# v with pixels on partitions, pixel blocks turned on VectorE, and another pacing of the taps in an attention and involution kernel

## The chip, the cores and the metric

One NeuronCore of a Trainium2 chip runs the kernel; the other cores are idle. The metric is the device time of one execution in microseconds. The engines are TensorE (PE), VectorE (DVE), ScalarE (ACT), GpSimd (POOL) and SyncE (SP), which here only issues DMAs. They run in parallel, each through its own list of instructions in order.

## What is computed

Two layers on an image batch of 4 x 512 channels x 64 x 64 pixels in fp32. The first is self-attention over the 4096 pixels of an image with 128 channels for q, k and v. The second is an involution, a 7x7 convolution whose weights are made per pixel and are shared by groups of 16 channels.

```python
# layer 0
q = einsum('oc,bcn->bon', wq, x) + bq        # 128 x 4096 per image, k and v alike
attn = softmax(einsum('bci,bcj->bij', q, k), axis=-1)
x = einsum('oc,bcn->bon', wo, einsum('bcj,bij->bci', v, attn)) + bo + x
# layer 1
o1 = relu(conv1x1(x, W1) * s1 + b1)          # 512 -> 128 channels
w  = conv1x1(relu(conv1x1(o1, Wr) * sr + br), Ws) + bs    # 49 taps x 8 groups per pixel
o2[c] = sum over 49 taps of w[tap, group of c] * (o1 shifted by the tap)[c]
x = conv1x1(o2, W3) * s3 + b3 + x
```

## The kernel before

**Layout.** Channels stand on partitions. An image is worked in eight chunks of 512 pixels (8 rows of 64). `fast_path` does all the work. `general_path`, which is built into the program too, runs only if the softmax sums leave a safe range, and isn't touched.

**Keys and values** (`keys_values`, L420). Once for each image, chunks 2 to 7, then 1 and 0. PE makes `pk` with four 512-column matmuls of the k weights on x, and ScalarE writes it to `kt` with the bias. PE makes `pv` in the same way, with channels on partitions; ScalarE copies it to `vs`; one chunk later `turn` lets PE transpose it in four pieces (`pvt`), and ScalarE copies that to `vT`, which has pixels on partitions as the second attention matmul needs it. The bias of v is added to the output bias (`bo`) instead.

**Attention** (`attention`, L576). For each block of 512 queries, 32 steps: a score matmul of 512 columns (`pss`), exp on ScalarE into one of five `pt` buffers, a value matmul into `po`, and DVE's sum of the `pt` into `pacc` in PSUM. The score runs two steps ahead. The last chunk of the last image is worked in two halves.

**After a block** (`finish_block`, L473). DVE makes the row sums, PE spreads them (`pl`), DVE scales; four matmuls `pwo` (L511) with the residual addition on DVE (L513); then `p1` from the sum, `o1` on ScalarE. `o1` is transposed on PE in four pieces (`pp`, L541), copied to `o1t`, and written to a DRAM scratch `pix` with two DMAs (L548), pixels by channels with zero margins. `pr` and `red` are the input of the involution's weights. The block adds two units of four image rows to `units`.

**The involution** (`involution`, L280). The `ring` in SBUF holds twelve image rows, loaded from `pix` by `pump` (L219) with two DMAs for each group of rows, seven shifted copies of a row side by side. For a unit, PE makes the weights (`pw`), DVE multiplies ring rows by weights (`prod`, L330, four buffers), and GpSimd adds into `acc` (L354). An operation takes n = 1 to 4 of the seven tap rows at once. `turn_unit` transposes the sum (`pa`), and `close_chunk` makes `py` and adds it to x on DVE (L408), after which x goes out. In the tail, after the last attention step, PE takes every second addition (`accp`), since it has nothing else to do.

**What sets the order.** A planner written out in the kernel. It counts PE's time in `pe` (`PE_COLUMN` for each column) and estimates when the others are free in `free`. `finish_block`, `turn_unit`, `close_chunk` and `involution` are generators. `chores` (L248) runs after every two matmuls of k or v and after every attention step, which is about 1.7 us of PE. It moves one step in `finishing`, one in `closing`, and then calls `pace` (L212), which places tap operations as long as PE's time has earned them (1.56 tap rows per us, not more than two operations a call). A tap operation is put off while the planned times of DVE or GpSimd lie too far ahead of PE's (3.5 and 7.5 us, L310) or while the ring rows it needs are not planned to have landed. A wait in a generator is a `yield`. All DMAs but one are issued by SP, and a scheduler places them between each other.

**The lead-in.** SP loads the k weights, then the first chunk of x in four parts, then the v weights; ScalarE loads the small vectors (L171). GpSimd sets `ones` (L180).

Of the kernel before, what the change touches and what calls it, by code (L numbers as in the profile page):

```python
# [8 lines left out]
F32 = mybir.dt.float32  # L9
# [4 lines left out]
B, C, H, W = 4, 512, 64, 64  # L14
N = H * W
P = 128
# [52 lines left out]
DVE_TAPS, POOL_TAPS = (0.16, 0.27), (0.19, 0.55)  # L69
ROW_US, X_US, PIX_US, LAND_US = 2.2, 3.8, 1.5, 3.0  # L70
HOP_US = 0.8
TB = 32

SAFE = (1e-30, 1e20)

# [2 lines left out]
def fast_path(  # L78
# [69 lines left out]
    reds, sums_c = {}, {}  # L148
    written = {}
    landing = {}  # L150
    low, load = 0, 0

    def until(us):
# [3 lines left out]
    def pe_us(us):  # L157
        nonlocal pe
        pe += us
# [8 lines left out]
        nc.sync.dma_start(xs[b, c], x_r[b, :, :, c * CH : (c + 1) * CH])  # L168


    nc.scalar.dma_start(vec, vecs)  # L171
    nc.sync.dma_start(wt[:, :O_WV], wts[:, :O_WV])
    c0, c1 = KEYS[:2]
    xs = {(0, c0): xpool.tile([P, CT, CH], F32, tag="x", name=f"x_0_{c0}")}
    for t in range(CT):
# [1 line left out]
    nc.sync.dma_start(wt[:, O_WV:O_WQ], wts[:, O_WV:O_WQ])  # L177
    load_x(0, c1)
    nc.sync.dma_start(wt[:, O_WQ:], wts[:, O_WQ:O_WR])
    nc.gpsimd.memset(ones, 1.0)  # L180
    make_identity(nc, ident)
    nc.gpsimd.memset(zero, 0.0)
    for i in range(P // TB):
# [8 lines left out]
    def w_slice(off, t):  # L192
        return wt[:, off + t * P : off + (t + 1) * P]
# [17 lines left out]

    def pace():  # L212
        nonlocal due, seen
        due, seen = min(due + TAPS_A_US * (pe - seen), 20), pe
        for _ in range(2):
            if due < 2 or not step(taps, 1):
                break

    def pump():  # L219

        nonlocal load
        while load // STEP in written:
            b, row = divmod(load, STEP)
            rows, us = written[b]

            end = H + SR - UR if rows == H else rows + PAD - 1
            n = min(b * STEP + end, low + RING) - load
            n = min(n, RING - load % RING)
            if n <= 0:
                break  # L230
            for h in range(2):
                src = pix[b % 2][row + h : row + h + n, :W, :]
                windows = bass.AP(
                    tensor=src.tensor, offset=src.offset, ap=[[P, W], [WP * P, n], [1, K * P]]
                )
                nc.sync.dma_start(
                    ring[h * W : (h + 1) * W, load % RING : load % RING + n]
                    .rearrange("p r x c -> p r (x c)"),
                    windows,
                )  # L240
            free["dma"] = max(free["dma"], us)
            us = takes("dma", ROW_US * n) + LAND_US
            landing.update((load + i, us) for i in range(n))
            load += n
            if row + n == H + SR - UR:
                load = (b + 1) * STEP
# [33 lines left out]
    def involution():  # L280
        nonlocal low, due
        while True:
# [15 lines left out]
            for o, (x, dy, n) in enumerate(ops):  # L298
                if o and dy >= DYS[1][0] > ops[o - 1][1]:
                    low = base + UR  # L300
                    pump()
                    if tail and units:
                        early[units[0]] = weights(*units[0])
                rows = [(base + dy + t * 2) % RING for t in range(NT)]
                while base + dy + n + NT > load:
                    yield "wait"
                landed = max(landing[base + dy + i] for i in range(n + NT))
                while not tail and (
                    pe < max(begin, landed)
                    or free["dve"] > pe + 3.5  # L310
                    or free["pool"] > pe + 7.5
                ):
                    yield "wait"
                free["pool"] = max(free["pool"], takes("dve", DVE_TAPS[0] + DVE_TAPS[1] * n))
                takes("pool", POOL_TAPS[0] + POOL_TAPS[1] * n)
                due -= n
                d0 = dy - DYS[dy >= DYS[1][0]][0]
                first = x == 0 and dy < DYS[1][0]
                prod, p0 = acc, d0
                if not first:  # L320
                    prod, p0 = prods.tile(
                        [P, NT, 4, P], F32, tag="prod", name=f"prod_{b}_{u}_{o}"
                    ), 0
                col = (x * K + dy) * G
                lines = ring[:, rows[0] : rows[0] + n, x, :]
                image = bass.AP(
                    tensor=lines.tensor, offset=lines.offset,
                    ap=[lines.ap[0], [(rows[1] - rows[0]) * K * P, NT], [K * P, n], [1, P]],
                )
                nc.vector.tensor_tensor(  # L330
                    prod[:, :, p0 : p0 + n, :].rearrange("p t d (g c) -> p t d g c", g=G),
                    image.rearrange("p t d (g c) -> p t d g c", g=G),
                    pw[:, :, col : col + n * G].unsqueeze(3)
                    .broadcast_to([P, NT, n * G, GC])
                    .rearrange("p t (d g) c -> p t d g c", d=n),
                    ALU.mult,
                )
                if first:
                    pass
                elif tail and o % 2 and (accp is not None or n > 1):  # L340

                    begin_sum = accp is None
                    if begin_sum:
                        accp = ps1.tile(
                            [P, NT, 2, P], F32, tag=("po", "acc")[u % 2], name=f"accp_{b}_{u}"
                        )
                    for d in range(0, n, 2):
                        k = min(2, n - d)
                        mm(
                            accp[:, :, :k, :], ident, prod[:, :, d : d + k, :],  # L350
                            begin_sum and d == 0, o + 2 >= len(ops) and d + 2 >= n,
                        )
                else:
                    nc.gpsimd.tensor_tensor(  # L354
                        acc[:, :, d0 : d0 + n, :], acc[:, :, d0 : d0 + n, :], prod[:, :, :n, :],
                        ALU.add,
                    )
                yield
# [61 lines left out]
    def keys_values(b):  # L420
        kt = kvpool.tile([P, N], F32, tag="k", name=f"k_{b}")
        vT = kvpool.tile([P, N // P, P], F32, tag="v", name=f"v_{b}")

        def turn(c, vs):
            pvt = ps1.tile([P, 4, P], F32, tag="acc", name=f"pvt_{b}_{c}")
            for j in range(4):
                nc.tensor.transpose(pvt[:, j, :], vs[:, j * P : (j + 1) * P], ident)
            pe_us(0.5)
            nc.scalar.copy(vT[:, 4 * c : 4 * c + 4, :], pvt)

        last = None
        for i, c in enumerate(KEYS):
            for k in KEYS[i + 1 : i + 3]:
                if (b, k) not in xs:
# [12 lines left out]
            nc.scalar.activation(  # L447
                kt[:, c * CH : (c + 1) * CH], pk, AF.Identity, bias=v1(V_BK)
            )
            if last is not None:  # L450
                turn(*last)
            pv = ps1.tile([P, CH], F32, tag="po", name=f"pv_{b}_{c}")
            for t in range(CT):
                mm(pv, w_slice(O_WV, t), xt[:, t, :], t == 0, t == CT - 1)
                if t % 2:
                    chores()
            vs = work2.tile([P, CH], F32, tag="q", name=f"vs_{b}_{c}")
            nc.scalar.copy(vs, pv)
            last = c, vs
        turn(*last)  # L460
        return kt, vT

    def queries(b, c, off, n):
# [9 lines left out]
    def finish_block(b, c, off, n, po, sums):  # L473
# [35 lines left out]
        for t in range(CT):  # L509
            pw = ps.tile([P, CH], F32, tag="mm", name=f"pwo_{name}_{t}")[:, :n]  # L510
            mm(pw, w_slice(O_WO, t), on)  # L511
            takes("dve", DVE_OP * n / CH)
            nc.vector.scalar_tensor_tensor(  # L513
                xt[:, t, :], pw, bo[:, t : t + 1], xt[:, t, :], ALU.add, ALU.add
            )
            for _ in range(t % 2 if late else 1 + (t != 1)):
                yield
        p1 = ps.tile([P, CH], F32, tag="mm", name=f"p1_{name}")[:, :n]
        for t in range(CT):
            mm(p1, w_slice(O_W1, t), xt[:, t, :], t == 0, t == CT - 1)  # L520
# [5 lines left out]
        def last_bias():  # L526

            for t in range(CT):
                nc.scalar.activation(xt[:, t, :], xt[:, t, :], AF.Identity, bias=v1(V_B3 + t))  # L529
                if t % 2:  # L530
                    yield

        if late:
            yield from until(pe + HOP_US)
        else:
            yield from last_bias()

        tiles = n // P
        pp = ps.tile([P, CH // P, P], F32, tag="mm", name=f"pp_{name}")[:, :tiles]
        for t in range(tiles):  # L540
            nc.tensor.transpose(pp[:, t, :], o1[:, t * P : (t + 1) * P], ident)  # L541
        pe_us(0.5)
        o1t = work1.tile([P, CH // P, P], F32, tag="o1t", name=f"o1t_{name}")[:, :tiles]
        nc.scalar.copy(o1t, pp)
        top = c * RW + off // W
        for h in range(2):
            row = PAD + top + h
            nc.sync.dma_start(  # L548
                pix[b % 2][row : row + 2 * tiles - 1 : 2, PAD : PAD + W, :]
                .rearrange("r w c -> w r c"),  # L550
                o1t[h * W : (h + 1) * W],
            )
        us = takes("dma", PIX_US) + LAND_US

        pr = ps.tile([P, CH // NT], F32, tag="mm", name=f"pr_{name}")[:, : n // NT]
# [77 lines left out]

    taps = [involution()]
    for b in range(B):
        kv = keys_values(b)
        if b == 0:

            pb = ps.tile([P, CT], F32, tag="mm", name="pb")
# [412 lines left out]
```

## Time and profile before

| | us |
|---|---|
| median of 14 runs | 2659.97 |
| lowest and highest | 2654.53, 2663.03 |
| the profiled execution | 2660.41 |
| its span, first to last instruction | 2658.6 |
| mean granted TensorE clock | 0.996 |

The stretches of the span, from the trace. The four attention stretches are long and even; between them lie the image changes, in which k and v of the next image are made while the last blocks of the old one are finished.

| stretch, us | what | PE busy | DVE busy | POOL busy |
|---|---|---|---|---|
| 0 to 66 | k and v of image 0 | 60.86 | 0.00 | 2.66 |
| 66 to 625 | attention 0 | 558.60 | 384.91 | 338.08 |
| 625 to 702 | change to image 1 | 74.57 | 40.95 | 64.21 |
| 702 to 1268 | attention 1 | 566.00 | 419.64 | 404.41 |
| 1268 to 1350 | change to image 2 | 78.94 | 42.85 | 67.03 |
| 1350 to 1912 | attention 2 | 562.00 | 416.61 | 400.69 |
| 1912 to 1998 | change to image 3 | 81.51 | 43.78 | 69.23 |
| 1998 to 2555 | attention 3 | 556.60 | 417.91 | 402.24 |
| 2555 to 2658.6 | end | 89.50 | 81.33 | 66.67 |

How to read it: an fp32 matmul shows as two records (x2 in the lists), each with a weight load of its own on the line PEld. Matmuls are pipelined and the length of one record includes its drain, so the time a matmul costs is the distance to the next one's start and not its length. Idle time of an engine stands in brackets, with the instruction whose end released it.

### The profile page before, as it was taken

How to read it: one execution, taken by the hardware profiler on the slowest of the kernel's cores; microseconds unless marked ns; L12 is line 12 of the kernel's file. 1: busy time of each engine (PE TensorE's matmuls, PEld its weight loads, DVE VectorE, ACT ScalarE, POOL GpSimd, SP SyncE). 2: the span in 40 equal slices, each digit the busy share in tenths (PEclk: the TensorE clock that was granted, in tenths of full speed). 3: DMA queues.
4: the chain of work that ended last, by engine and by line, in shares of the span. 5: the costliest groups of instructions: out<-in, count | busy, mean ns of one | idle time of the engine just before them, and what ended most of it. 6: DMA issues, size and time to landing. Idle time of an engine off the chain costs nothing.

```text
span 2658.6 us, 22780 instructions
## 1 busy us (share of the span) xinstructions
PE 2628.6 (99%) x6834; PEld 1200.0 (45%) x6834; DVE 1848.0 (70%) x2601; ACT 886.5 (33%) x1486; POOL 1815.2 (68%) x1195
## 2 busy tenths in 40 slices
PE   9999999999999999999999999999999999999998
PEld 4444444444444444444444444444444444444574
DVE  0347788786665777778565678778747577777877
ACT  2333333332333333333233333333323333333330
POOL 0007788788852878878774487878778277888865
PEclk9999999999999999999999999999999999999999
DMA  6032322235604233333440433333452423322243
GB/s 231 0 73 60 90 69 76 61 71 137 159 32 105 60 91 91 91 91 78 126 127 20 89 72 76 91 91 91 107 153 70 105 60 91 78 57 58 56 99 99
DMA packets 104259, 231.59 MB, mean 87 GB/s; under 512 B 5240, under 2 KB 23872, under 8 KB 104000
## 3 DMA queue, kind: packets, MB, share of 16 engines
q1 hardware_dynamic: 103984, 229.96, 35.1%
q8 instruction: 55, 0.90, 0.1%
q14 instruction: 76, 0.62, 0.1%
q10 hardware_dynamic: 144, 0.10, 0.0%
HBM read 187.28 MB, written 42.77 MB: 87 GB/s over the span
## 4 chain that ended last, share of the span: by engine, by line
PE 91%; POOL 4%; DMA 2%; DVE 2%; issue 1%; SPq 0%; ACT 0%; POOLq 0%; DVEq 0%; ACTq 0%
PE pss L200 33%; PE po L200 33%; PE p L200 4%; PE py L200 4%; PE pwo L200 4%; PE pq L200 4%; POOL acc L354 4%; PE pv L200 2%; PE pk L200 2%; PE pw L200 2%; DMA ring<-pix 1%; DVE prod L330 1%; PE accp L200 1%; PE pr L200 1%; DMA out_dram<-x 1%
## 5 line engine op out<-in xcount | busy, mean ns | idle before, releaser
L354 POOL TENSOR_TENSOR acc<-acc,prod 128x768 f32<-128x768 f32 (+3 forms) x1060 | 1693.3, 1616 | 818.1 <-DVE prod L330 632.9
L200 PE MATMUL pss<-q,k 128*128 128x512 f32 (+1 forms) x2112 | 1059.0, 586 | 0.0
L200 PE MATMUL po<-pt,v 128*128 128x512 f32 (+1 forms) x2112 | 1047.2, 580 | 0.0
L594 ACT ACTIVATE pt<-pss 128x512 f32<-128x512 f32 x1024 | 611.2, 597 | 1226.3 <-PE pss L200 1198.4
L625 DVE TENSOR_TENSOR pacc<-pacc,pt 128x512 f32<-128x512 f32 x958 | 666.2, 695 | 472.6 <-ACT pt L594 466.1
L330 DVE TENSOR_TENSOR prod<-ring,pw 128x512 f32<-128x512 f32 (+3 forms) x1092 | 899.3, 849 | 108.2 <-POOL acc L354 62.1
L200 PEld LDWEIGHTS po<-pt,v 128*128 128x128 f32 x2112 | 399.6, 190 | 478.4 <-issue 459.2
L200 PEld LDWEIGHTS pss<-q,k 128*128 128x128 f32 x2112 | 390.1, 190 | 455.8 <-issue 447.2
L408 DVE SCALAR_TENSOR_TENSOR x<-py,vec,x 128x512 f32<-128x512 f32 (+1 forms) x132 | 96.5, 732 | 64.5 <-PE py L200 62.2
L200 PE MATMUL py<-accT,wt 128*128 128x512 f32 (+1 forms) x264 | 132.8, 587 | 0.7 <-ACT accT L393 0.5
L200 PE MATMUL pwo<-on,wt 128*128 128x512 f32 (+1 forms) x264 | 129.9, 585 | 0.1
L200 PE MATMUL p<-x,wt 128*128 128x512 f32 (+1 forms) x264 | 121.4, 588 | 7.3 <-DVE x L513 7.3
L365 POOL TENSOR_TENSOR acc<-acc 128x512 f32<-128x512 f32 x120 | 119.8, 998 | 9.4
L200 PE MATMUL pk<-x,wt 128*128 128x512 f32 x256 | 119.6, 605 | 4.8 <-DMA x<-x_dram 4.8
L529 ACT ACTIVATE x<-x,vec 128x512 f32<-128x512 f32 (+1 forms) x132 | 92.9, 706 | 91.8 <-PE p L200 86.9
L200 PE MATMUL pv<-x,wt 128*128 128x512 f32 x256 | 116.8, 594 | 0.0
L200 PE MATMUL pq<-x,wt 128*128 128x512 f32 (+1 forms) x264 | 115.9, 580 | 0.0
L330 DVE TENSOR_TENSOR acc<-ring,pw 128x1024 f32<-128x1024 f32 (+1 forms) x84 | 79.1, 961 | 47.1 <-PE pw L200 47.1
L513 DVE SCALAR_TENSOR_TENSOR x<-pwo,bo,x 128x512 f32<-128x512 f32 (+1 forms) x132 | 96.0, 732 | 22.3 <-PE pwo L200 20.4
L200 PEld LDWEIGHTS p<-x,wt 128*128 128x128 f32 x264 | 50.3, 191 | 68.1 <-issue 56.0
L200 PEld LDWEIGHTS pwo<-on,wt 128*128 128x128 f32 x264 | 51.2, 194 | 61.4 <-issue 55.8
L200 PEld LDWEIGHTS pk<-x,wt 128*128 128x128 f32 x256 | 48.8, 194 | 64.5 <-issue 58.8
(58 smaller groups left out, 799.7 us busy)
## 6 DMA issues: line engine op xcount, KB each, us to landing
x<-x_dram SPq DMA_DIRECT2D x55, 1024.0 KB, 5.7
ring<-pix SPq DMA_DIRECT2D x32, 1344.0 KB, 15.3
ring<-pix SPq DMA_DIRECT2D x72, 448.0 KB, 8.6
out_dram<-x SPq DMA_DIRECT2D x31, 1024.0 KB, 4.2
ring<-pix SPq DMA_DIRECT2D x32, 896.0 KB, 13.4
ring<-pix SPq DMA_DIRECT2D x8, 2240.0 KB, 25.1
pix<-o1t SPq DMA_DIRECT2D x62, 128.0 KB, 2.5
ring<-pix SPq DMA_DIRECT2D x8, 224.0 KB, 3.2
```

The costliest lines, as they stand in the source:

```text
L200: return nc.tensor.matmul(o, lhsT=lhsT, rhs=rhs, start=start, stop=stop)
L330: nc.vector.tensor_tensor(prod[:, :, p0 : p0 + n, :].rearrange("p t d (g c) -> p t d g c", g=G), image.rearrange("p t d (g c) -> p t d g c ...
L354: nc.gpsimd.tensor_tensor(acc[:, :, d0 : d0 + n, :], acc[:, :, d0 : d0 + n, :], prod[:, :, :n, :], ALU.add,)
L365: nc.gpsimd.tensor_tensor(acc[:, :, :n, :], acc[:, :, :n, :], acc[:, :, n : 2 * n, :], ALU.add)
L408: nc.vector.scalar_tensor_tensor(xt[:, t, :], py, v1(V_S3 + t), xt[:, t, :], ALU.mult, ALU.add)
L513: nc.vector.scalar_tensor_tensor(xt[:, t, :], pw, bo[:, t : t + 1], xt[:, t, :], ALU.add, ALU.add)
L529: nc.scalar.activation(xt[:, t, :], xt[:, t, :], AF.Identity, bias=v1(V_B3 + t))
L594: nc.scalar.activation(pt, pss, AF.Exp)
L625: nc.vector.tensor_tensor(paccs[k], paccs[k], pt, ALU.add)
```

## The change

It has eight edits in `fast_path`:

- **v**: `keys_values` makes `pv` with x as the stationary operand and the v weights as the moving one: 16 matmuls of 128 columns for a chunk. The result has pixels on partitions, so `turn`, its transposes and `vs` go. The PSUM bank alternates between two tags.
- **Pixel blocks** of images 0 to 2 are turned by DVE in blocks of 32x32, right after `o1`, and not by PE. Eight DMAs write them, one for each of four channel groups and two column halves, with runs of 32 channels (128 bytes). They are placed after the last bias and three more `yield`s. Image 3 keeps the old way.
- **p1** of images 0 to 2 comes two `yield`s later.
- **pace** may place 2 + int(elapsed PE time / 1.0 us) operations in a call instead of two.
- **Lag**: the limit on GpSimd's planned time is 4.0 us while k and v are made and 7.5 in attention. DVE's limit in the last image is 4.5.
- **Ring loads** of the last image take at most three rows at once.
- **Lead-in**: the k weights are issued by ScalarE in two parts ahead of the vectors, so that SP's first DMA is x.
- **Lead-in matmuls**: DVE sets `ones`, and eight 128x128 matmuls on it run before the first data are there; their result isn't used.

```diff
+POOL_LAG = 4.0, 7.5
+PIECE = 3
+WARM = 8
...
+    for cols in (slice(0, P), slice(P, O_WV)):
+        nc.scalar.dma_start(wt[:, cols], wts[:, cols])
     nc.scalar.dma_start(vec, vecs)
-    nc.sync.dma_start(wt[:, :O_WV], wts[:, :O_WV])
...
-    nc.gpsimd.memset(ones, 1.0)
+    nc.vector.memset(ones, 1.0)
+
+    warm = ps.tile([P, P], F32, tag="mm", name="warm")
+    for _ in range(WARM):
+        nc.tensor.matmul(warm, lhsT=ones, rhs=ones, start=True, stop=True)
...
+        steps = 2 + int((pe - seen) / STEP_US)
         due, seen = min(due + TAPS_A_US * (pe - seen), 20), pe
-        for _ in range(2):
+        for _ in range(steps):
...
-            n = min(n, RING - load % RING)
+            n = min(n, RING - load % RING, PIECE if b == B - 1 else RING)
...
-                    or free["dve"] > pe + 3.5
-                    or free["pool"] > pe + 7.5
+                    or free["dve"] > pe + (4.5 if b == B - 1 else 3.5)
+                    or free["pool"] > pe + lag
...
-            if last is not None:
-                turn(*last)
-            pv = ps1.tile([P, CH], F32, tag="po", name=f"pv_{b}_{c}")
-            for t in range(CT):
-                mm(pv, w_slice(O_WV, t), xt[:, t, :], t == 0, t == CT - 1)
-                if t % 2:
+            pv = ps1.tile([P, 4, P], F32, tag=("po", "acc")[i % 2], name=f"pv_{b}_{c}")
+            for j in range(4):
+                for t in range(CT):
+                    mm(
+                        pv[:, j, :], xt[:, t, j * P : (j + 1) * P], w_slice(O_WV, t),
+                        t == 0, t == CT - 1,
+                    )
+                if j % 2:
                     chores()
-            vs = work2.tile([P, CH], F32, tag="q", name=f"vs_{b}_{c}")
-            nc.scalar.copy(vs, pv)
-            last = c, vs
-        turn(*last)
+            nc.scalar.copy(vT[:, 4 * c : 4 * c + 4, :], pv)
...
+        for _ in range(0 if late else 2):
+            yield
         p1 = ps.tile([P, CH], F32, tag="mm", name=f"p1_{name}")[:, :n]
...
         else:
+
+            blocks = o1t.rearrange("p t c -> p (t c)")
+            takes("dve", DVE_OP)
+            nc.vector.transpose(
+                blocks.rearrange("p (k q) -> p k q", q=TB), o1.rearrange("p (k q) -> p k q", q=TB)
+            )
             yield from last_bias()
+            for _ in range(3):
+                yield
+            for i in range(P // TB):
+                channels = slice(i * TB, (i + 1) * TB)
+                for h in range(W // TB):
+                    columns = slice(PAD + h * TB, PAD + (h + 1) * TB)
+                    nc.sync.dma_start(
+                        pix[b % 2][PAD + top : PAD + top + RW, columns, channels]
+                        .rearrange("r a c -> a r c"),
+                        blocks[channels].rearrange("p (r h c) -> p r h c", r=RW, c=TB)[:, :, h, :],
+                    )
...
     for b in range(B):
+        lag = POOL_LAG[0]
         kv = keys_values(b)
+        lag = POOL_LAG[1]
```

More of the change, by code (lines that the diff above doesn't have):

```diff
@@ L71 @@
 HOP_US = 0.8
+STEP_US = 1.0
+POOL_LAG = 4.0, 7.5
+PIECE = 3
 TB = 32
+WARM = 8
 SAFE = (1e-30, 1e20)
@@ L150, in fast_path @@
     landing = {}
+    lag = 0.0
     low, load = 0, 0
@@ L422, in keys_values @@
         vT = kvpool.tile([P, N // P, P], F32, tag="v", name=f"v_{b}")
[L424 to L431, printed above, removed]
         for i, c in enumerate(KEYS):
@@ L531, in last_bias @@
                     yield
+        tiles = n // P
+        top = c * RW + off // W
+        o1t = work1.tile([P, CH // P, P], F32, tag="o1t", name=f"o1t_{name}")[:, :tiles]
         if late:
             yield from until(pe + HOP_US)
-        else:
-            yield from last_bias()
[L538 to L552, printed above, removed]
+            pp = ps.tile([P, CH // P, P], F32, tag="mm", name=f"pp_{name}")[:, :tiles]
@@ new lines, in finish_block @@
+            for t in range(tiles):
+                nc.tensor.transpose(pp[:, t, :], o1[:, t * P : (t + 1) * P], ident)
+            pe_us(0.5)
+            nc.scalar.copy(o1t, pp)
+            for h in range(2):
+                row = PAD + top + h
+                nc.sync.dma_start(
+                    pix[b % 2][row : row + 2 * tiles - 1 : 2, PAD : PAD + W, :]
+                    .rearrange("r w c -> w r c"),
+                    o1t[h * W : (h + 1) * W],
+                )
+        else:
+            blocks = o1t.rearrange("p t c -> p (t c)")
[3 more added lines that the diff above has]
+            )
+            yield from last_bias()
+            for _ in range(3):
[4 more added lines that the diff above has]
+                    columns = slice(PAD + h * TB, PAD + (h + 1) * TB)
+                    nc.sync.dma_start(
+                        pix[b % 2][PAD + top : PAD + top + RW, columns, channels]
+                        .rearrange("r a c -> a r c"),
+                        blocks[channels].rearrange("p (r h c) -> p r h c", r=RW, c=TB)[:, :, h, :],
+                    )
```

## The prediction, made before the changed kernel was run

> **What bounds the kernel now.** I read the page first, for the engines; then the list of PE's waits, the chain of waits at the lead-in, and the timelines of PE, VectorE (DVE) and SyncE (SP) where an image ends.
>
> ```profile
> PE 2628.6 (99%) x6834; PEld 1200.0 (45%) x6834; DVE 1848.0 (70%) x2601; ACT 886.5 (33%) x1486; POOL 1815.2 (68%) x1195
> ```
>
> PE is busy all the time, DVE and GpSimd (POOL) are not. A microsecond of PE work that goes is a microsecond of time, as long as nothing else becomes late. Where PE stands still it is for these reasons (total us, times, longest):
>
> ```profile
> PE p L200 <- DVE x L513: 7.3, 3, 2.4
> PE pk L200 <- DMA x<-x_dram: 4.8, 1, 4.8
> ...
> PE pw L200 <- DVE prod L330: 2.7, 2, 2.1
> ```
>
> Prices come from the chain (start, us, what; x8 records are four fp32 matmuls, two passes each):
>
> ```profile
> 4.81 6.29 PE pk L200 x8
> ...
> 14.53 3.43 PE pk L200 x8
> 17.96 0.44 PE pvt L427 x4
> 18.40 3.44 PE pv L200 x8
> ...
> 65.77 0.59 ACT vs L458
> ...
> 671.00 0.44 PE pp L541 x4
> ...
> 2646.25 2.69 PE pa L200 x24
> ```
>
> The first k chunk takes 6.29 us where every later one takes 3.43. The four v transposes of a chunk cost 0.44, those of a pixel block (pp) also 0.44. The last line is the only place in which 128-column fp32 matmuls with a new stationary operand each run back to back (line 391): 2.69/24 = 0.112 us a pass, against 3.44/32 = 0.1075 for the same 128 columns in a 512-column pass.
>
> PE's timeline at the second and third image change:
>
> ```profile
> 1302.82 2.91 PE L200 MATMUL p<-x,wt 128*128 128x512 f32 x4 [2.43 <-DVE x L513]
> 1305.52 1.83 PE L200 MATMUL py<-accT,wt 128*128 128x512 f32 x2
> 1307.19 0.60 PE L427 MATMUL pvt<-ident,vs 128*128 128x128 f32 x4
> ...
> 1996.52 1.60 PE L200 MATMUL pw<-wt,red 33*128 33x392 f32 x4 [2.06 <-DVE prod L330]
> 1998.06 5.49 PE L200 MATMUL pss<-q,k 128*128 128x512 f32 x6
> ```
>
> The stall is in brackets, but the price goes on behind it: py takes 1.67 us to the next start where two records take 0.86 elsewhere. And the reason for the wait, on DVE, with where the ring comes late:
>
> ```profile
> 654.55 0.95 DVE L330 TENSOR_TENSOR prod<-ring,pw 128x768 f32<-128x768 f32 x1 [1.47 <-POOL acc L354]
> ...
> 695.31 2.28 DVE L330 TENSOR_TENSOR prod<-ring,pw 128x256 f32<-128x256 f32 x5 [8.05 <-DMA ring<-pix]
> ```
>
> DVE works in order. Products that wait for GpSimd to free one of four buffers stand ahead of the residual addition (line 513) that the p matmul needs.
>
> **What the Trainium skill says.** "TensorE: Matmul & The Clock Gate", section on LDWEIGHTS: a load takes its columns divided by 1.2 GHz, 107 ns for 128, and overlaps the running matmul; so a 128-column fp32 pass is just long enough to hide the next load. The 0.112 us above agrees. Same page, Part 1: after an idle window of about 3.4 us the clock falls to half until it has been busy for one. Here stalls of 2.43 and 2.06 us were followed by passes of double length, and the first chunk ran so too. "VectorE: DVE Perf Modes", The three transpose paths: DVE transposes only 32x32 blocks; this is why the pixel rows then need DMAs by block. "DMA: Bandwidth & Descriptors", Specifications: writes below 512 B are read-modify-write. The changed pixel writes have runs of 128 B; no row of this trace shows such a write.
>
> **Part by part, on the profiled execution (2660.4 us, span 2658.6; the median is 2660.0, so the result is read against either).**
>
> 1. v. 32 chunks lose their transposes: 32 x 0.44 = -14.1. In their place 16 matmuls of 128 columns do what 4 of 512 did: 32 passes x 0.112 = 3.58 against 3.44, +0.15 x 32 = +4.8. Net **-9.3**. Bounds of the pass: 0.1075 (nothing lost, -14) to 0.190, PEld's mean load time, if loads were not hidden (+80); I take 0.112 because that row is the same form. ScalarE loses a copy per chunk. PSUM banks alternate, so pv does not wait for its copy of 0.59. The wait for the last chunk's copy at 65.8 (0.7 us idle) goes: **-0.8**.
>
> 2. Pixel blocks of images 0 to 2: 24 x 0.44 = **-10.6** of PE. DVE gains 24 transposes at the 0.723 us of its 128x512 transpose (spread, line 502), 17 us on an engine at 70%. The two DMAs of a block become eight. SP spends 0.63 us on each (two in 1.25):
>
> ```profile
> 600.61 1.25 SPq L548 DMA_DIRECT2D pix<-o1t  x2
> 603.24 0.37 SPq L168 DMA_DIRECT2D x<-x_dram  x1
> 603.97 0.60 SPq L236 DMA_DIRECT2D ring<-pix  x1
> ```
>
> So the pixels land about 6 x 0.63 = 3.8 us later, plus what the short runs cost (0 to 4). Behind them on SP stand the ring loads, and for those the products. The change gives three further steps (about 1.7 us of PE each) between the transpose and these DMAs in the plan, so the planner also places the products some 5 us later. I take nothing in the middle of an image.
>
> 3. Image changes. Two extra steps before p, and a limit of 4.0 instead of 7.5 us on GpSimd's planned lag while k and v are made. In the order of DVE's instructions three of the four additions then stand directly behind one another with no product between, the last one four products after pw of unit 12, and p's second half 17 us of PE work after that pw. So the three stalls go: 3 x 2.43 = 7.3. With them the slow clock behind the second and third: p 2.70 against 1.82 to the next start, py 1.67 against 0.86, 1.7 each, 3.4 in all. **-10.7**. The wait of pw (2.06 and 0.63) goes too: pw of unit 14 moves from before the first score to after the 11th step, some 20 us later. With it goes the slow clock: pw 1.54 against 0.86, six score records 5.27 against 2.57. **-6.1**.
> What comes late next: unit 13 needs ring rows of the last block. Before, they landed at 695.2, ten us before the first score at 705. From the new order I count the DVE transpose some 28 us before the first score, eight writes (about 9 us), then the ring loads (18.3 us from pixels to the second load before): they land at about the first score. The softmax sums queue behind those products on DVE, five pt buffers of 1.72 us cover 8.6 us. That is used up nearly; I charge 2 us a change, **+6** (0 to 18).
>
> 4. Lead-in. x is issued at once, in SP's first slot (0.74 instead of 1.20), the weights come by ScalarE's queue, and eight 128-column matmuls on ones run from about 1.05 us, 16 passes at half clock, 0.213 each, until 4.5. So the first k matmul starts at about 4.5 instead of 4.8, and the clock is full earlier; depending on when the busy window closes the chunk ends at 7.9 to 9.6, against 11.1. I take 8.8: **-2.3**.
>
> 5. End. Planned lag of DVE 4.5, ring loads of three rows. In DVE's order eight products of unit 12 (seven with n = 4 at 1.2 us, one at 0.95) move ahead of the last block's sums; before, all of that unit stood after them (its first product is at 2569.15). DVE sets the pace after that, 72 of 90 us busy in the stretch from 2569. 9.3 less about 3 for the sums that now come later: **-6.5** (0 to -10).
>
> Sum: -9.3 - 0.8 - 10.6 - 10.7 - 6.1 + 6 - 2.3 - 6.5 = -40.3. **2660 - 40 = 2620 us.**
>
> **Rivals.** (a) The stalls at image changes only move: the ring rows stand in for the residual, and 10.7 + 6.1 come back: 2637. For it speaks the 8.05 us that DVE waits now and the later pixels; against it the distance of pw and p from what they need in the new order. (b) Everything fits, nothing for the ring and the whole gain at the end: 2620 - 6 - 3 = 2611. (c) Slower: short writes hold up SP. If the pixels land more than the five pt buffers' 8.6 us behind the plan, PE stops at every block. The gain of 40 is used up at 40/24 = 1.7 us of stall a block; writes that end 12 us late would give 3.4 x 24 = 82, so 2702. Against it: 2.5 us from issue to landing now, DMA engines 35% busy, and the three steps of cover. (d) Slower too: weight loads not hidden, 1024 passes x (0.190 - 0.112) = 80: 2700. The row at 2646 speaks against it.
>
> **How the numbers follow.** The forecast 0.50 (2614 to 2628), (a) with its partial forms 0.27 (2628 to 2645), (b) 0.15, (c) 0.04, (d) 0.02, no change 0.02. Below 0.2% (5 us) a change can't be told from none. Faster 0.92, same 0.02, slower 0.06. The range 2605 to 2643 leaves out (c), (d) and the edges of (a) and (b).
>
> **What would show it.** A k and v chunk pair of 7.0 us instead of 7.3 in the lead-in; pv passes of 0.112; no pp in the first three images; no wait of p on x and none of pw on prod; the first k chunk ending near 8.8; pixel writes landing within 10 us of the transpose, and DVE's waits for the ring under about 10 us each; the stretch from the last po to the end about 82 us instead of 88. Wrong would be: pv passes near 0.19, pss waiting for pt at the first steps of an image, or ring waits in the middle of an image.

## The result, and the profile after

The changed kernel takes 2623.73 us, median of six runs (2623.34 to 2625.91), against 2659.74 for the kernel before (28 runs, 2652.02 to 2663.32); the ratio is 0.9869, 95% interval 0.9859 to 0.9878. So it is faster by 1.3%, and the 2620 of the prediction is 3.7 us too low. The profiled execution has a span of 2621.6 us against 2658.6: 37.0 us less where 40.3 were summed up. Cut into stretches, with the terms of the prediction sorted into the same ones (an image change is from the first `pk` of an image to its first `pss`):

| stretch, us | before | after | predicted | measured |
|---|---|---|---|---|
| start to first score | 72.23 | 66.49 | -5.4 | -5.7 |
| four attention stretches | 2252.42 | 2242.02 | -9.3 | -10.4 |
| three image changes | 245.96 | 233.67 | -19.1 | -12.3 |
| last `po` to end | 88.00 | 79.41 | -6.5 | -8.6 |
| sum | 2658.6 | 2621.6 | -40.3 | -37.0 |

Only one stretch falls behind its forecast, the image changes. PE's list of waits after (total us, times, longest) shows how:

```profile
PE py L210 <- DVE x L419: 6.7, 3, 2.4
PE accp L210 <- DVE prod L341: 2.4, 1, 2.4
PE pss L210 <- ACT q L471: 2.3, 3, 0.8
```

The waits of `p` on x and of `pw` on `prod`, which led the list before, are gone. Two new ones stand in their place, three times each, once a change. (The `accp` line is in the tail.) The timeline of the second change of the kernel after shows the first of them (start, us, engine, operation, count, in brackets the idle time and what ended it):

```profile
1288.99 1.88 PE L210 MATMUL p<-x,wt 128*128 128x512 f32 x4
...
1290.71 1.02 PE L210 MATMUL py<-accT,wt 128*128 128x512 f32 x2
...
1293.28 1.88 PE L210 MATMUL p<-x,wt 128*128 128x512 f32 x4
...
1295.45 0.95 DVE L341 TENSOR_TENSOR prod<-ring,pw 128x768 f32<-128x768 f32 x1 [0.94 <-POOL acc L365]
...
1297.34 0.95 DVE L341 TENSOR_TENSOR prod<-ring,pw 128x768 f32<-128x768 f32 x1 [0.94 <-POOL acc L365]
1298.21 0.74 DVE L419 SCALAR_TENSOR_TENSOR x<-py,vec,x 128x512 f32<-128x512 f32 x1
...
1299.01 1.12 PE L210 MATMUL py<-accT,wt 128*128 128x512 f32 x2 [2.13 <-DVE x L419]
```

Products that wait for GpSimd stand ahead of an addition again, as before. But it is now an addition of `py` (L419), in the same chain, and what waits is not a reader of x: the third `py` of the chunk waits for the addition of the second, which is made 6.5 us after that one's matmuls. All that it can need from there is the PSUM buffer. `p` and `py` share two of them (tag `mm` of the pool `ps`), and here `p`, whose halves lie ahead of and behind the second `py`, holds the other one.

The wait of `p` in the kernel before was one for a buffer too, and not for x, as the prediction reads it. From its timeline at the same change:

```profile
1295.08 1.02 PE L200 MATMUL pwo<-on,wt 128*128 128x512 f32 x2
...
1302.02 0.74 DVE L513 SCALAR_TENSOR_TENSOR x<-pwo,bo,x 128x512 f32<-128x512 f32 x1
...
1302.82 2.91 PE L200 MATMUL p<-x,wt 128*128 128x512 f32 x4 [2.43 <-DVE x L513]
```

The first half of `p` reads only the first two of the four parts of x, whose additions were made at 1283.70 and 1287.97. It waited for the fourth, of the last `pwo`. (In one of the kernels below, with `p` early and the limit at 7.5, that half starts at 1284.93 while the fourth addition runs from 1284.72 to 1285.47, so it doesn't need its result.)

The second new wait, in the timeline of after at the first change:

```profile
694.17 0.69 ACT L471 ACTIVATE q<-pq,vec 128x512 f32<-128x512 f32 x1 [2.85 <-PE pq L210]
694.91 2.51 PE L210 MATMUL pss<-q,k 128*128 128x512 f32 x5 [0.78 <-ACT q L471]
```

With `pw` moved away nothing is left on PE between the `pq` matmuls and the first score, so the copy of q (0.69 us) lies open. To the start of the next record PE takes 1.37 us there and 0.43 elsewhere: 0.94 a change.

The lead-in and the pixel writes, from the timeline of after:

```profile
1.06 3.78 PE L190 MATMUL warm<-ones 128*128 128x128 f32 x16 [1.06 <-DVE ones L186]
...
4.63 4.13 PE L210 MATMUL pk<-x,wt 128*128 128x512 f32 x8
...
8.60 3.73 PE L210 MATMUL pv<-wt,x 128*128 128x128 f32 x32
...
12.18 1.02 PE L210 MATMUL pk<-x,wt 128*128 128x512 f32 x2
```

The first k chunk ends at 8.60 and not at 10.94. The 32 passes of `pv` take 12.18 - 8.60 = 3.58 us, 0.112 each. The page of after gives, for the engines and for the writes (count, KB each, median us from issue to landing):

```profile
PE 2599.0 (99%) x7382; PEld 1240.4 (47%) x7382; DVE 1865.1 (71%) x2626; ACT 857.2 (33%) x1430; POOL 1821.5 (69%) x1197
...
pix<-o1t SPq DMA_DIRECT2D x192, 32.0 KB, 1.7
```

DVE has taken over the turning and is at 71% instead of 70%; ScalarE has lost 29 us of copies. Each of the eight short writes lands no later, at the median, than the two long ones did (2.5).

### The profile page after: what moved, and what is told of

It reads as the page before. It is cut to its first block, busy times and chain, and to the rows that moved or that the text cites. A ratio compares the mean times of both kernels' runs of the same rounds, so it can differ in the third digit from the quotient of the medians.

```text
span 2621.6 us, 24098 instructions
## 1 busy us (share of the span) xinstructions
PE 2599.0 (99%) x7382; PEld 1240.4 (47%) x7382; DVE 1865.1 (71%) x2626; ACT 857.2 (33%) x1430; POOL 1821.5 (69%) x1197
## 2 busy tenths in 40 slices
DMA packets 143898, 231.70 MB, mean 88 GB/s; under 512 B 57032, under 2 KB 63632, under 8 KB 143632
## 5 line engine op out<-in xcount | busy, mean ns | idle before, releaser
L210 PEld LDWEIGHTS pv<-wt,x 128*128 128x128 f32 x1024 | 121.8, 195 | 15.8 <-issue 15.3
L210 PE MATMUL pv<-wt,x 128*128 128x128 f32 x1024 | 123.3, 279 | 0.0
L419 DVE SCALAR_TENSOR_TENSOR x<-py,vec,x 128x512 f32<-128x512 f32 (+1 forms) x132 | 95.8, 726 | 29.6 <-PE py L210 28.0
L210 PEld LDWEIGHTS py<-accT,wt 128*128 128x128 f32 x264 | 49.1, 190 | 65.5 <-issue 48.5
L210 PEld LDWEIGHTS pq<-x,wt 128*128 128x128 f32 x264 | 49.8, 190 | 58.7 <-issue 56.4
## 6 DMA issues: line engine op xcount, KB each, us to landing
ring<-pix SPq DMA_DIRECT2D x74, 448.0 KB, 10.6
```

Of the source, the lines that this page charges most:

```text
L210: return nc.tensor.matmul(o, lhsT=lhsT, rhs=rhs, start=start, stop=stop)
L419: nc.vector.scalar_tensor_tensor(xt[:, t, :], py, v1(V_S3 + t), xt[:, t, :], ALU.mult, ALU.add)
```

## Experiments

Each kernel is the changed kernel with the edit shown. All but one were run once, on three chips; the changed kernel itself varied by 2.6 us over its six runs, so I read differences below that from the trace alone.

**Two parts undone: v, and the pixel blocks.** The first puts the old `pv`, `turn` and `vs` back in `keys_values`:

```diff
-            pv = ps1.tile([P, 4, P], F32, tag=("po", "acc")[i % 2], name=f"pv_{b}_{c}")
+            pv = ps1.tile([P, CH], F32, tag="po", name=f"pv_{b}_{c}")
...
+            vs = work2.tile([P, CH], F32, tag="q", name=f"vs_{b}_{c}")
+            nc.scalar.copy(vs, pv)
+            last = c, vs
```

> The changed kernel with v made and transposed as before. If PE is the bound and parts add up, the span is 2621.6 + 14.1 - 4.8 = 2631 us, and up to 1 us more for the wait on the last copy. If GpSimd and DVE are what sets the length of the middle, PE's extra work hides in their shadow and the span stays under 2626.

Measured 2628.92 us. To the first score it takes 69.98 instead of 66.49, so undoing costs 3.5 us in the lead-in, where the prediction had 2.3 + 0.8 for the eight chunks. But the other 24 chunks, at the three changes, cost only 1.6 together (235.27 against 233.67), and not 7.0. PE's waits in this kernel say where the rest is:

```profile
PE py L210 <- DVE x L419: 4.1, 3, 1.4
```

The wait is 2.6 us shorter than in the kernel after, and the clock never falls behind it, which is another 3.4. So with the old v, PE reaches `py` later, DVE's addition is then nearly due, and 1.6 + 2.6 + 3.4 = 7.6 us are about the 7.0. The time that the new v saves at a change was handed on to a wait.

The second undoes the blocks on DVE: all images use PE's transposes, one ScalarE copy and two writes, and the three steps ahead of the writes go too.

```diff
-            nc.vector.transpose(
-                blocks.rearrange("p (k q) -> p k q", q=TB), o1.rearrange("p (k q) -> p k q", q=TB)
-            )
...
+            nc.tensor.transpose(pp[:, t, :], o1[:, t * P : (t + 1) * P], ident)
```

> The changed kernel with the pixel blocks of images 0 to 2 turned on PE and written by two DMAs, without the three steps. If only PE's 24 x 0.44 count, the span is 2621.6 + 10.6 = 2632 us. If the eight writes cost something at the image changes (late ring rows), this kernel gives it back and the span is 2624 to 2628. If the steps around the writes are what removed the wait of pw, that wait returns, with up to 6 us more: 2638.

Measured 2630.96 us. The three attention stretches concerned are longer by 3.30 us each, 9.9 in all, 7 x 3 blocks at 0.47: the price of the prediction (0.44) was right, and the removal is hidden behind nothing there. The changes are shorter by 2.3 us together, since PE's wait for `py` falls to 5.1 + 1.1 us and the clock stays up.

**What I had credited with the end of p's wait.** First the lower limit on GpSimd's lag undone, then the two extra steps ahead of `p1`, then both.

```diff
-POOL_LAG = 4.0, 7.5
+POOL_LAG = 7.5, 7.5
```

> The changed kernel with GpSimd's lag limit at 7.5 us throughout. If the limit removed the wait of p on x (three times 2.4 us and the slow clock behind), that wait returns and the span is 2626 to 2632. If the two extra steps before p removed it, PE shows no wait of p on x and the span stays within 2 us of 2621.6.

```diff
-        for _ in range(0 if late else 2):
-            yield
```

> The changed kernel with p at its old place, lag limit 4.0 kept. If the two steps removed the wait of p on x, it returns here, about 2.4 us at each of three changes: 2626 to 2632. If the lag limit did, there is no such wait and the span stays within 2 us of 2621.6. In either case the new wait of py on DVE should move, since py then stands elsewhere against the products.

> The changed kernel with two parts undone: p directly behind the residual addition as before (no two extra steps), and the limit on GpSimd's planned lag 7.5 us throughout. Theory one, the lag limit alone is what keeps products from standing ahead of the residual addition: with it gone the p matmul waits on that addition again, some 2.4 us at each of three changes, with slow clock behind some of them (1.7 us each): 2617 + 7 to 12 = 2624 to 2629 us, and the wait of p on x at the top of PE's list. Theory two, the limit decides nothing at these places (it changed nothing where the two steps stood): 2617 us like the run with p early, no wait of p on x.

Measured: 2623.34, 2617.03 and 2624.34 us. The limit alone does nothing, the steps alone cost 6.5 us, and both undone give the time of the changed kernel. In none of the three does `p` wait for an addition. What is decided is the wait of `py`. First the kernel with p early and the low limit:

```profile
PE py L210 <- DVE x L419: 0.4, 1, 0.4
```

and the kernel with both undone:

```profile
PE py L210 <- DVE x L419: 7.7, 3, 3.1
```

So my expectation for the last run got the time right and the name wrong: 7 us more, but as a wait of `py`. Both theories fall in part. With p early, it is the first `py` that stands between the halves of `p`, and the second that takes its buffer. The addition in question is made 4.6 to 4.9 us after the matmuls of the first `py` with the low limit, nearly in time, and 6.6 to 7.6 us after them with 7.5. So there the low limit is needed. With p two steps later the limit moves the addition little (6.5 to 6.8 us after the second `py`, 6.4 to 6.6 with 7.5), and `py` waits either way.

**Pacing by PE's time.** The extra operations in a call of `pace` undone:

```diff
-        steps = 2 + int((pe - seen) / STEP_US)
+        steps = 2
```

> The changed kernel, with at most two products per call of the pacing function as before, not more when more PE time has passed. Theory one: products are paced by their due time, PE never waits for them in mid-image, so nothing moves: 2623 us within 2. Rival: the extra steps let the products of a long stretch of PE work catch up before the image change; without them more products stand ahead of the residual addition there and the wait of py on x grows, or the last image ends with products left over: 2627 to 2633 us.

Measured 2616.71 us, 7 us faster than with them, on the side that neither theory had. The wait of `py` is gone from PE's list. The timeline of this kernel at the second change, to be held against the one above:

```profile
1286.98 1.88 PE L210 MATMUL p<-x,wt 128*128 128x512 f32 x4
...
1290.42 1.88 PE L210 MATMUL p<-x,wt 128*128 128x512 f32 x4
...
1292.13 1.02 PE L210 MATMUL py<-accT,wt 128*128 128x512 f32 x2
...
1296.49 1.02 PE L210 MATMUL py<-accT,wt 128*128 128x512 f32 x2
...
1298.77 1.37 DVE L419 SCALAR_TENSOR_TENSOR x<-py,vec,x 128x512 f32<-128x512 f32 x2
```

The addition for the second `py` (1292.13) is still late: it is made at 1298.77, 5.6 us after the matmuls and behind three products, as in the kernel after. But the third `py` starts at 1296.49, ahead of that addition and with no bracket, so it takes the other buffer. Both halves of `p` now stand ahead of the second `py`, which the planner places later against `p`, and the buffer of `p` is free. All 14 traces agree, up to the last `po`: a `py` starts before the addition for the one ahead of it has ended 108 times, always with nothing between the two in these buffers, and never in the 331 places where a half of `p` lies between. All 30 waits of `py` for L419 at the changes are among these.

Each change takes 74.28 us (after: 78.65, 76.68, 78.34), 10.8 less in sum, most of it the 6.7 us of idle and two stretches of slow clock (3.4). Against that stand 2.4 more at the end, 0.9 in attention and 0.8 in the lead-in (there the first k chunk ends at 9.38 instead of 8.60; no tap operation runs yet, so this is not the edit's doing). So the extra steps earn some 3.3 us in attention and at the end, and cost three times that at the changes, by the place that they give to `py`. They don't do it alone: with them kept and `p` two steps earlier (2617.03) nearly all of the wait is gone as well. The same kernel with the lag limit at 7.5 throughout:

> The changed kernel with at most two products per call of the pacing function, and the limit on GpSimd's planned lag 7.5 us throughout. Theory one: the lower limit was only needed against the products that the extra steps let through, so without those steps it decides nothing: 2616 to 2618 us, no wait of py or p on x. Rival: the limit holds the products back in either case; with 7.5 us the queue of products on DVE is deep enough again to hold up a residual addition: 2621 to 2626 us with a wait of py or p on x of about 2.4 us a change.

It took 2616.80 us with no such wait. Without the extra steps the limit decides nothing; the first theory holds. In neither of the two pairs that hold the two later steps for `p1` (2623.34 and 2623.73, 2616.80 and 2616.71) did it move the time.

**The wait for q.** The queries of an image's first block are made before the last `pv`, not after it:

```diff
+            if i == NCH - 1:
+                first = queries(b, 0, 0, CH)
...
-        qs[0] = queries(b, *blocks[0])
+        qs[0] = first
```

> The changed kernel, with the queries of an image's first block made before the last v chunk and not after it. Theory one: the first score waits for the copy of q, about 0.94 us at each of three image changes, because nothing stands between the q matmul and it; with the last v chunk (3.6 us of PE) in between the wait goes: 2623.4 - 2.8 = 2620.6 us, no wait of pss on q. Rival: the score is held up by something else as well (the last k copy, or the ring), and the wait only changes its name: 2623 us.

Measured 2620.26 us, span 2618.4 against 2621.6, and the wait is not in the list any more. Then both gains in one kernel, run five times:

> The changed kernel with at most two products per call of the pacing function, and with the queries of the first block made before the last v chunk: the two edits that gained alone. Theory one: they remove different waits (py on x, 6.6 us with the slow clock behind it; pss on q, 3.2 us), so they add up: 2623.4 - 6.6 - 3.2 = 2613.6 us, with neither wait in PE's list. Rival: with q earlier the products at the image change shift again and part of the py wait comes back: 2615 to 2620 us.

It took 2614.27 us (2613.44 to 2616.19), ratio to the kernel before 0.9834, interval 0.9821 to 0.9848, which lies wholly below that of the changed kernel. The gains add up to within 1 us. Its timeline at the first change shows q copied under the last v chunk and the first score without a bracket:

```profile
684.77 1.88 PE L210 MATMUL pq<-x,wt 128*128 128x512 f32 x4
686.49 3.73 PE L210 MATMUL pv<-wt,x 128*128 128x128 f32 x32
686.69 0.69 ACT L473 ACTIVATE q<-pq,vec 128x512 f32<-128x512 f32 x1 [2.75 <-PE pq L210]
690.06 2.41 PE L210 MATMUL pss<-q,k 128*128 128x512 f32 x5
```

**The three steps ahead of the writes.** Undone alone:

```diff
             yield from last_bias()
-            for _ in range(3):
-                yield
```

> The changed kernel without the three further steps between the DVE transpose and the eight writes of a pixel block. Theory one: the steps are cover only for SP's queue, which stands still on a write that waits for its transpose, with x and ring loads behind it; the landing is planned by time in either case and TensorE waits for none of it: 2623 us within 2. Rival one, the cover is needed: ring rows or x come late, waits of DVE on the ring grow over 5 us a change and TensorE waits for pt or x: 2628 to 2640 us. Rival two: rows land some 5 us earlier, the products at the image change start earlier and TensorE's wait of py on x shrinks: 2617 to 2621 us.

Measured 2645.97 us: 22 us slower than the changed kernel, over half of what the change gains. The timeline of this kernel at the second change, of SP and in the last line of PE:

```profile
1308.17 3.78 SPq L567 DMA_DIRECT2D pix<-o1t  x8
1312.36 0.39 SPq L428 DMA_DIRECT2D out_dram<-x  x1
1313.40 3.31 SPq L247 DMA_DIRECT2D ring<-pix  x4
1316.75 0.60 SPq L173 DMA_DIRECT2D x<-x_dram  x1
...
1333.23 6.34 PE L210 MATMUL pk<-x,wt 128*128 128x512 f32 x8 [4.44 <-DMA x<-x_dram]
```

And SP's timeline of the kernel after:

```profile
1300.83 2.79 SPq L569 DMA_DIRECT2D pix<-o1t  x6
1303.74 0.39 SPq L173 DMA_DIRECT2D x<-x_dram  x1
1304.17 0.99 SPq L569 DMA_DIRECT2D pix<-o1t  x2
1305.38 0.40 SPq L428 DMA_DIRECT2D out_dram<-x  x1
1310.14 12.94 SPq L247 DMA_DIRECT2D ring<-pix  x6
```

With the steps, the load of x slips in between the eight writes, ahead of `out` and the ring. Without them it stands in SP's queue behind all eight, the output and four ring loads. Counted from the first `pk` of the change, it is issued 53.5 us in instead of 48.6, and it then shares the DMA engines with the ring rows: PE can go on 16.5 us after its issue, having waited 4.44, where in the kernel after the load landed 5.7 us after its issue. Two windows of half clock come with each such wait. All three changes show it (16.1 us of waiting for x in all). So rival one holds, at a price above its range. DVE's waits for the ring grow as it said, to 6.48, 5.52 and 6.26 us; what PE waits for is x.

**The end, and the lead-in.** Ring loads not cut to three rows, DVE's limit at 3.5 in the last image too:

```diff
-            n = min(n, RING - load % RING, PIECE if b == B - 1 else RING)
+            n = min(n, RING - load % RING)
...
-                    or free["dve"] > pe + (4.5 if b == B - 1 else 3.5)
+                    or free["dve"] > pe + 3.5
```

> The changed kernel, with the end as before: ring loads not cut to three rows in the last image, planned lag of DVE 3.5 us there too. Theory one: these two settings make the gain at the end; from the last po to the end it takes 88.0 us again instead of 79.4: 2632 us. Rival: part of it comes from products that are further along for other reasons (pacing, the writes of the blocks): the stretch is 82 to 85 us, 2626 to 2629 us.

Measured 2626.86 us, in the rival's range, but from the last `po` to the end 81.35, below both theories. Most of the rest is chance at the changes (235.25 against 233.67): all three `py` waits have a stretch of half clock behind them there, in the kernel after two. The windows of this stretch (length, then busy us and instructions of PE, PEld, DVE, ACT, POOL; clock, DMA share, GB/s), of the kernel after:

```profile
2542.20:2621.60 79.40, 67.36 (x257) 38.49 (x255) 63.81 (x90) 7.33 (x16) 51.51 (x32) 0.97 0.35 91
```

of this kernel:

```profile
2543.70:2625.10 81.40, 67.91 (x261) 38.48 (x260) 65.84 (x93) 7.33 (x16) 52.07 (x33) 0.97 0.34 93
```

and of the kernel before:

```profile
2570.60:2658.60 88.00, 73.90 (x273) 42.13 (x271) 70.65 (x96) 7.66 (x17) 54.43 (x33) 0.94 0.33 85
```

DVE is at work for all but 15.6 to 17.4 us in each. What changes is how much is left for it: 70.65, 65.84, 63.81. The two settings account for 2.0 of these 6.8; another 4.8 was already ahead of the last `po` without them. The paced steps, undone, lengthen the stretch by 2.4; which edit brings the rest was not separated.

The lead-in matmuls left out (`WARM = 0`):

> The changed kernel without the lead-in matmuls on ones. Theory one: the lead-in matmuls are what brings TensorE to full clock before the first k chunk; without them the chunk runs its first 3.4 us at half clock and ends about 1.7 to 2.1 us later, from 8.60 to 10.3 to 10.7, and everything after it as well: 2625.1 to 2625.6 us. Rival: the earlier issue of x and of the weights by another queue makes the gain of the lead-in, the clock is not decisive: chunk end 8.6 to 9.2, 2623.4 to 2624 us.

The first k chunk runs from 4.35 to 9.40, so it ends 0.80 later than in the kernel after: between the two theories. But this one run doesn't price the matmuls. In the twelve kernels that have them the chunk ends anywhere from 8.38 to 9.38, and the clock first rises at 3.99 to 7.27 us (here at 7.43). The time, 2622.40, isn't longer, for a reason that has nothing to do with the lead-in; it is the first point of the last section.

## Why the prediction was right, and where not

The forecast of faster was right and the time within its range, since most of its terms have the right sign and about the right size, and two errors offset each other in part: a wait not foreseen at the changes, and a charge for the ring that was not spent. Point by point:

- **v (-9.3 and -0.8).** The price of a pass was right, 0.112, and the weight loads are hidden. In the lead-in undoing it cost 3.5. At the changes, the same saving came out as waiting. That it reaches the time once the wait of `py` is gone fits the last paragraph of this section, but no run has the old v without that wait. Rival (d) falls.
- **Pixel blocks (-10.6).** Right: 9.9 for the attention part against 9.2. That the later pixels cost nothing in mid-image was right, and holds without the three steps too (four attention stretches of 2241.8 us there, 2242.0 after). I took the steps for cover of the planner. They decide the order on SP's queue at the image changes, and are worth 22 us. The mechanism of rival (c), SP held up, was real; I had looked for it in the ring rows of every block and not in the loads of x at the changes.
- **Image changes (-10.7, -6.1, +6).** This is the step that failed. I took `p`'s wait for one for x, and counted how far `p` stands from the additions that it reads. It was a wait for a PSUM buffer that an addition was to free. It went for `p`, but the additions of `py` stand behind the same products, and the third `py` needs the buffer that one of them frees. That wait cost 6.7 us and 3.4 of slow clock, about all of the 10.7. Rival (a), stalls that only move, named the effect, with the ring as its cause; the cause is that the second `py` stands between the halves of `p` while products hold up its addition. Undoing the extra steps of `pace` or the two later steps of `p1` moves it out of there (2616.71 and 2617.03 us); with `p` earlier the first `py` comes to stand there instead, but the addition for it is nearly in time. The reason that I gave for the end of `p`'s wait was wrong as well: without the two later steps and the lower limit `p` does not wait either. No kernel of these runs has its wait back, so which edit removed it is open. The -6.1 for `pw` held, but the same move uncovered the copy of q, 3 x 0.94 = 2.8, which I hadn't asked for. The +6 for the ring was not spent: DVE's waits for the ring at the changes are 3.51, 2.73 and 2.26 us, and PE sees none of them. Summed up again, -7.0 (v) - 1.3 (blocks) - 10.7 - 6.1 + 10.1 + 2.8 = -12.2, where -12.3 was measured.
- **Lead-in (-2.3).** Measured -2.34, so close by luck: with the lead-in matmuls the chunk's end varies by 1.0 us from kernel to kernel, and 8.60 is one value of these. What the matmuls bring of it is not shown.
- **End (-6.5).** Measured -8.6. I credited it to the two settings of the last image; they bring 2.0.

The kernel with both new waits removed takes 73.34 us a change, 25.9 less than before in sum. My terms without the ring's +6 give 25.1. (In attention that kernel takes 3.1 us more than the kernel after, at the end 2.2 more.) So the work at the changes was counted about rightly, and its order wrongly.

## What to carry to other kernels

A wait that is put down to an addition need not be for its result: `p` and `py` waited for the buffer that it was to free. Ask which buffers are held by a sum that is worked in two halves, and what is placed between the halves. When a wait is removed, go through every instruction behind the same queue, and every buffer that these release, before counting the gain; a saving ahead of a wait that another engine sets comes out as a longer wait. A DMA queue's order is part of the schedule: eight writes instead of two are cheap or cost 22 us depending on which side of the next load they stand.

## What the runs showed of the hardware

**The clock falls by fixed windows.** The windows (length, PE busy, clock, DMA share, GB/s) round the three `py` waits of the kernel after:

```profile
657.16:660.57 3.41, 0.97 (x3) 1.00 0.00 0
660.57:663.99 3.42, 3.42 (x11) 0.50 0.12 19
1295.45:1298.86 3.41, 1.43 (x4) 1.00 0.00 0
1298.86:1302.28 3.42, 3.27 (x23) 1.00 0.09 18
1933.74:1937.15 3.41, 1.25 (x5) 1.00 0.00 0
1937.15:1940.57 3.42, 3.42 (x18) 0.50 0.24 38
```

Slow stretches begin a whole number of 3.413 us windows after the first rise of the clock (192, 566 and 745 in this run), and each of these lasts one window. The Trainium skill, "TensorE: Matmul & The Clock Gate", Part 1, says that the window is 3413 ns and runs freely; the trace agrees. It names an idle window as what drops the clock; here 1.25 busy of 3.41 us was enough, and 1.43 was not. Over the stalls at image changes of all runs that began at full clock, idle of 2.06 us or more within one window was followed by half clock, and up to 1.98 us was not. This is no threshold for the whole kernel: after the last `po`, windows with as little as 1.10 us of idle (in the kernel with two operations a call) were followed by half clock too, and others with up to 1.72 us were not. So whether a stall of 2.2 us costs 1.7 more depends on where it falls: the kernel without the lead-in matmuls has one such stretch at its changes where the kernel after has two, and so it isn't slower. The spread of the lead-in, where the first rise came anywhere within 3.28 us (3.99 to 7.27), fits a window that runs freely as well.

**Short writes.** The Trainium skill, "DMA: Bandwidth & Descriptors", Specifications, has transfers below 512 B done by read-modify-write; no run here shows how they are done. The 128-byte runs raise the packets under 512 B from 5240 to 57032, and a write of 32 KB lands in 1.7 us at the median; SP spends 0.45 us on each. DVE's waits for ring rows, which are read back from these pixels, are no longer than before (10.0 us in all, 44.6 before). The cost that the runs show is the places that the writes take in SP's queue.
